# Multi-head latent attention block: query weights loaded two pairs ahead, projection pieces at other heads, first output products moved forward

## The chip, the core and the metric

The kernel runs on one core of a Trainium2 chip. The metric is the device time of one launch in microseconds; smaller is better. Five engines work side by side, each on its own list of instructions in its own order: TensorE (PE in the profile, with its weight loads as PEld), VectorE (DVE), ScalarE (ACT), GpSimd (POOL) and SyncE (SP). SP does no arithmetic here; it issues transfers (DMA). A transfer or an instruction that has to wait holds up all that stands behind it in the list of the same engine.

## The reference

One transformer block on a sequence of 2048 tokens with 512 features: attention with low-rank queries and keys (16 heads, query rank 384, key and value rank 128, 128 plain and 64 rotary features per head), a residual sum and layer norm, then a linear layer with bias, a residual sum and layer norm again. Cut to what matters:

```python
cq = rms_norm(x @ w_qa.T, q_a_ln_w)                  # 2048 x 384
q = (cq @ w_qb.T).reshape(b, s, H, 192)              # 128 plain + 64 rotary per head
q_pe = q_pe * cos + rotate_half(q_pe) * sin
ckv = x @ w_kva.T                                    # 128 latent + 64 rotary, shared by the heads
kv = rms_norm(ckv[..., :128]) @ w_kvb.T              # keys and values of each head
scores = einsum('bhqd,bhkd->bhqk', q_full, k_full) * scale, causal
out = softmax(scores) @ v                            # then @ w_o.T
x = layernorm(x + out)
x = layernorm(x + x @ (w * scale_weight).T + bias)
```

All is float32 in and out. The kernel never builds keys and values per head: the key half of `w_kvb` is multiplied into the query weights once, the value half into the output weights, so scores and values work on the 128-wide latent that all heads share.

## The kernel before, in words

To keep float32 accuracy on a faster matmul, most operands are split in a high and a low part (`split`, L60: a copy on ACT, the difference on DVE), and a product is three matmuls.

The 2048 queries go through in four blocks `b` of 512, and in each block the 16 heads go through as eight pairs `p`. A pair has four query tiles `qt` of 128 queries, so eight steps, called heads below: head 0 is tile 0 of the first head (`j` = 0), head 1 is tile 0 of the second, and so on to head 7. `units` (L607) writes this order out. Block 0 takes a shorter path with a whole tile at a time, mixed with the projections of the input and of the weights; blocks 1 to 3 run in a region where the order on PE and SP is the order of the program (`manual_schedule`, L717), while a planner places the work of ACT, DVE and POOL.

In a head, `head_scores` (L418) computes the scores on PE (L407) into PSUM tiles `s`, the row maximum on DVE (L440), a bias, and the exponential on ACT (L455) into `pr`. `head_probs` (L471) scales and splits them into 16-bit halves `hl` (L476 on ACT, L479 on DVE), and SP transposes them by DMA (L483) into a ring in SBUF. It is a generator that is finished in the course of the next head, so the transpose of a head stands in SP's order after the next head's scores. `values` (L521) multiplies the transposed probabilities with the latent (L532) into a PSUM tile `o`; it runs some tiles later (`lag`), and its result goes through `ot` (L537, ACT) to DRAM (`ot_d`, L284 on POOL in block 0, L292 on SP later).

The queries of the next pair are made meanwhile, in pieces ("fillers") that `fill` (L543) takes one at a time between a head's scores and the values of an earlier tile:

- `project_nope` (L366): two pieces of nine matmuls each (L377), one per head of the pair, from `cq` (the block's 384-wide latent queries) and `wq` (the pair's weights, 768 KB). After the second piece it issues the load of the next pair's `wq` (`load_wq`, L309) into the same, single buffer; after the last pair's it also issues the load of the next block's `cq` and `cs` (`load_block`, L297).
- `project_pe` (L322): for four heads at once, two pieces of nine matmuls (L334) with the products with cosine and sine on DVE (L339). What follows (sums on POOL, copies and differences) is written by the third call, together with the next piece.

A pair with an even number has four pieces, one with an odd number two, the last pair of a block four (the next block's first pair). The heads after which a piece is taken, in block 1 before its last pair: 0, 1, 2, 4 (odd pairs 0, 1); in block 2 after its first pair 0, 1, 3, 5 (odd 0, 1); elsewhere 1, 3, 5, 7 (odd 1, 3). SP's list has the transposes, the loads of `wq`, `wpe`, `cq`, `cs`, and the stores `ot_d`, which `put_in` places.

In the last two pairs of block 3 the loads of the output weights start: `wv` and a quarter `wo0` (1 MB each) at pair 6, `wo1` at pair 7. `value_output` (L172) multiplies them to the combined weights `wvo` of a pair; pairs 0 and 1 are made as pieces of pair 7.

After the last head, `wo2` and `wo3` are loaded (L730), the outstanding values are finished (`finish`, L695), and the last stage begins: per pair, `latent` (L760) loads an `o` tile of the stored results (512 KB) and splits it (`oh`, `ol`), `accumulate` (L771) multiplies it with `wvo` into one of four PSUM tiles `acc` (six matmuls each), and layer norms and the linear layer are worked in between. In this stage only PE's order is written out; SP's is the planner's, which had moved the loads and splits of the first `o` tiles forward into pair 6 of block 3.

Of the kernel before, what the change touches and what calls it, by code (L numbers as in the profile page):

```python
# [11 lines left out]
F32 = mybir.dt.float32  # L12
# [7 lines left out]
P = 128  # L20
# [29 lines left out]
def mla_block(ctx: ExitStack, tc: tile.TileContext, a, out):  # L50
# [258 lines left out]
    def load_wq(b, p):  # L309
        if b == NB:  # L310
            return
        w = state["wq", b, p] = prj.tile([P, 2, LT, 256], F32R, tag="wq", name=f"wq{b}_{p}")
        c0 = (p % 2) * 256
        move(state["queue"], w, wq_d[p // 2][:, :, :, c0 : c0 + 256])
# [7 lines left out]
    def project_pe(b, g, direct=None):  # L322
# [6 lines left out]
        for x in range(2):  # L329
# [10 lines left out]
            if x:  # L340
                if b or g == 3:
                    load_wpe(*((b, g + 1) if g < 3 else (b + 1, 0)))
            yield
# [20 lines left out]
        state["pe", b, g] = pe  # L364

    def project_nope(b, p, direct=None):  # L366
# [5 lines left out]
        for j in range(2):  # L372
# [9 lines left out]
            if j == 1:  # L382
                state["qn", b, p] = qn
                if b or p == NPAIR - 1:
                    load_wq(*((b, p + 1) if p + 1 < NPAIR else (b + 1, 0)))
                if p == NPAIR - 1:
                    load_block(b + 1)
# [186 lines left out]
    wq0 = prj.tile([P, 2, LT, 256], F32R, tag="wq", name="wq0_0")  # L574
# [32 lines left out]
    def units(pool, ring, b):  # L607
        lag = min(ring.shape[1] // (2048 * (b + 1)) - 1, 3)

        for p in range(NPAIR):  # L610
            put_in(True)
            if b and p % 2 == 0 and p + 2 < NPAIR:
                fillers.append(project_pe(b, p // 2 + 1))
            if p + 1 < NPAIR:
                fillers.append(project(b, p + 1) if b == 0 else project_nope(b, p + 1))
            elif b + 1 < NB:
                fillers.append(project(b + 1, 0))
            if b == NB - 1 and p == NPAIR - 2:
                wv = state["wv"] = blk.tile([P, H, P], F32, tag="pe", name="wv")
                nc.sync.dma_start(wv, a["wv"])  # L620
                wo = state["wo"] = [pool.tile([P, 4, HID], F32, tag="wo", name="wo0", bufs=1)]
                nc.sync.dma_start(wo[0], a["wo"][:, 0:4])
            if b == NB - 1 and p == NPAIR - 1:
# [5 lines left out]
                wv, wo = state["wv"], state["wo"]  # L629
# [9 lines left out]
            for qt in range(4):  # L639
# [19 lines left out]
                else:  # L659
                    for j in range(2):  # L660
# [3 lines left out]
                        if (b, p, qt, j) == (1, 0, 0, 0):  # L664
                            half_values()
                            half_values()
                        early = b == 1 and p + 1 < NPAIR
                        if j != early or qt == 0 and (early or b == 2 and p > 0):
                            fill()
# [25 lines left out]
    def finish():  # L695
        flush()
        while vals:
            half_values()

# [10 lines left out]

    ctx_m = ctx.enter_context(ExitStack())
# [4 lines left out]
    state["queue"] = nc.sync  # L716
    with tc.manual_schedule(engines={mybir.EngineType.PE, mybir.EngineType.SP}):  # L717
        for b in range(1, NB):
            with ExitStack() as ctx_s:
# [4 lines left out]
                units(blk13, ring, b)  # L724
        put_in(True)
    state["queue"] = nc.gpsimd
    pcr, wvo, wv, wo = (state[k] for k in ("pcr", "wvo", "wv", "wo"))
    for i, tag in ((2, "pe"), (3, "qn")):
        wo.append(blk.tile([P, 4, HID], F32, tag=tag, name=f"wo{i}"))
        nc.sync.dma_start(wo[i], a["wo"][:, 4 * i : 4 * i + 4])  # L730
    ps_a = ctx.enter_context(tc.tile_pool(name="ps_a", bufs=4, space=PSUM, reuse_waits="tile"))
    finish()
# [10 lines left out]
    ohl = [[pc.tile([P, 4, 256], F32R, name=f"ohl{p}_{i}") for i in range(2)] for p in range(4)]  # L743
# [15 lines left out]

    def latent(b, p, last):  # L760
        o = pcr.tile([P, 4, 256], F32, tag="o", name=f"o{b}_{p}")
        nc.sync.dma_start(o, ot_d[b][p])
        if last and p >= 4:
            oh, ol = ohl[p - 4]
        else:
            oh = pcr.tile([P, 4, 256], F32R, tag="oh", name=f"oh{b}_{p}")
            ol = pcr.tile([P, 4, 256], F32R, tag="ol", name=f"ol{b}_{p}")
        split(o, oh, ol)
        return oh, ol

    def accumulate(acc, p, t, oh, ol):  # L771
        for j in range(2):
            c = slice(j * P, (j + 1) * P)
            for n, (l, i) in enumerate(((oh, 0), (oh, 1), (ol, 0))):
                nc.tensor.matmul(  # L775
                    acc,
                    l[:, t, c],
                    wvo[p][:, i, j, :],
                    start=p == 0 and j == 0 and n == 0,
                    stop=p == NPAIR - 1 and j == 1 and n == 2,  # L780
                )
# [30 lines left out]

    late = []
# [8 lines left out]
    with tc.manual_schedule(engines={ET.PE}):  # L822
        order = [(b, p) for b in range(NB) for p in range(NPAIR)]
        cuts = {order[0]: latent(0, 0, False)}
        for b in range(NB):
            last = b == NB - 1
            accs = [ps_a.tile([P, HID], F32, tag="acc", name=f"acc{b}_{t}") for t in range(4)]
            for p in range(CUT if last else NPAIR):
                nxt = order[NPAIR * b + p + 1]
                cuts[nxt] = latent(*nxt, nxt[0] == NB - 1)  # L830
                for t in range(4):
                    accumulate(accs[t], p, t, *cuts[b, p])
                    if b == 0 and p + 2 < NPAIR and t == 1:
                        heads = [2 * (p + 2) + j for j in range(2)]
                        for _ in value_output(
                            p + 2, wvo[p + 2], [wv[:, h] for h in heads], [wo[h // 4][:, h % 4] for h in heads], ps_f, "ff"
                        ):
                            pass
# [78 lines left out]
```

## Time and profile before

| what | value |
|---|---|
| median of 3 runs | 1662.82 us (1662.26 to 1666.56) |
| time of the profiled execution | 1661.02 us |
| its span | 1659.2 us |
| mean granted clock of TensorE | 0.981 |
| PE busy | 1567.8 us, 94% of the span |
| DVE, ACT, POOL busy | 71%, 56%, 20% |
| mean busy share of the DMA engines, 262 to 1390 us | about 0.78 |
| the same after 1413 us | 0.29 |

Block 0 ends near 257 us, block 1 near 524, block 2 near 909, block 3's last scores near 1384; the last values end at 1412.8. A row of the timeline gives the start, the length and the instruction, and in brackets the idle time of its engine before it with what ended it. A wait row reads "who waited, for whom: total, times, longest". An SP row's length holds the time that the queue took over the instruction, its waits too. PEclk is the clock that TensorE was granted, in tenths; it drops to half for some time around longer gaps.

### The profile page before, as it was taken

The page shows a single profiled execution, that of the slowest core. Times are in us where ns is not written, and L with a number is a line of the kernel's source. Part 1 is how long each engine was busy: PE and PEld are TensorE (multiplying, and loading weights), DVE is VectorE, ACT ScalarE, POOL GpSimd, SP SyncE. Part 2 cuts the span into 40 slices and gives each one's busy share as a digit, 9 for nine tenths or more (in the row PEclk, how much of TensorE's full clock was granted, in tenths as well). Part 3 has the DMA queues.
Part 4 walks back from the last instruction along what each step waited for, and adds up shares of the span by engine and source line. Part 5 has one row for each costly group of instructions (what it writes and reads, how often), then busy time and mean ns, then how long its engine had stood idle before and what let it go on. Part 6 is the DMA issues. An engine that isn't in the chain of part 4 may idle for free. (4 is left out here: it accounts for less than half of the span.)

```text
span 1659.2 us, 24718 instructions
## 1 busy us (share of the span) xinstructions
PE 1567.8 (94%) x9130; PEld 1299.4 (78%) x9130; DVE 1172.6 (71%) x2115; ACT 936.1 (56%) x1647; POOL 330.7 (20%) x404
## 2 busy tenths in 40 slices
PE   8998997999998799999998999999999997999997
PEld 7787876778777678888887888888888785788886
DVE  6777776777777868787786777767767774455464
ACT  5776765565556646666675656666566664312120
POOL 2332424143100505040000310500500000022132
PEclk9999998999999999999999999999999998999999
DMA  6979674878787767878887677787688998333230
GB/s 218 246 213 238 156 194 108 165 163 159 159 193 151 146 141 149 178 153 169 201 180 140 117 160 153 152 159 161 126 158 191 189 179 188 105 108 120 90 121 32
DMA packets 632841, 262.50 MB, mean 158 GB/s; under 512 B 570288, under 2 KB 611120, under 8 KB 631696
## 3 DMA queue, kind: packets, MB, share of 16 engines
q1 hardware_dynamic: 621184, 233.35, 64.7%
q0 software_dynamic: 4768, 17.99, 3.5%
q10 hardware_dynamic: 6768, 9.57, 1.9%
q8 instruction: 72, 1.18, 0.3%
q14 instruction: 49, 0.40, 0.1%
HBM read 83.17 MB, written 35.13 MB: 71 GB/s over the span
## 5 line engine op out<-in xcount | busy, mean ns | idle before, releaser
L407 PE MATMUL s<-Kn,qn 128*128 128x512 f32 (+4 forms) x1920 | 520.7, 377 | 12.2 <-ACT pr L455 10.3
L455 ACT ACTIVATE pr<-s,bias,rq 128x1024 f32<-128x1024 f32 (+3 forms) x320 | 324.1, 1016 | 194.2 <-DVE bias L449 150.4
L532 PE MATMUL o<-ring,V 128*128 128x256 f16 x3252 | 400.7, 277 | 27.7 <-DMA ring<-hl 18.2
L479 DVE SCALAR_TENSOR_TENSOR hl<-pr,inv,hl 128x1024 f16<-128x1024 f32 (+7 forms) x320 | 358.7, 1136 | 83.0 <-ACT hl L476 81.2
L532 PEld LDWEIGHTS <-V 128*128 128x128 f16 x3264 | 307.4, 99 | 117.6 <-issue 61.6
L476 ACT ACTIVATE hl<-pr,inv 128x1024 f16<-128x1024 f32 (+7 forms) x320 | 295.4, 961 | 182.6 <-DMA ring<-hl 74.9
L407 PEld LDWEIGHTS s<-Kn,qn 128*128 128x128 f32 x1920 | 338.7, 190 | 61.1 <-ACT pr L455 16.6
L440 DVE TENSOR_REDUCE neg<-s 128x1 f32<-128x1024 f32 (+3 forms) x320 | 318.5, 995 | 83.9 <-PE s L407 79.9
L407 PE MATMUL s<-Kp,pe 128*128 128x512 f32 (+4 forms) x1280 | 361.0, 363 | 0.0
L407 PEld LDWEIGHTS s<-Kp,pe 128*128 128x128 f32 x1280 | 234.0, 189 | 29.8
L377 PE MATMUL ps_qn<-cq,wq 128*128 128x512 f32 x576 | 151.9, 410 | 23.0 <-DMA wq<-wq_d 15.5
L346 POOL TENSOR_TENSOR prod<-prod 128x512 f32<-128x512 f32 x15 | 19.3, 1288 | 740.7 <-DVE prod L339 740.7
L377 PEld LDWEIGHTS ps_qn<-cq,wq 128*128 128x128 f32 x576 | 111.1, 198 | 47.6 <-issue 12.5
L775 PE MATMUL acc<-wvo,oh 128*128 128x512 f32 x448 | 143.5, 401 | 0.0
L361 POOL TENSOR_TENSOR pe<-prod,ph 32x512 fp32r<-32x512 f32 x76 | 119.7, 1575 | 10.0 <-issue 5.1
L775 PEld LDWEIGHTS acc<-wvo,oh 128*128 128x128 f32 x448 | 83.4, 188 | 20.9 <-issue 2.9
L775 PE MATMUL acc<-wvo,ol 128*128 128x512 f32 x224 | 88.4, 395 | 0.0
L284 POOL DMA_DIRECT2D ot_d<-ot x33 | 18.7, 568 | 293.8 <-ACT ot L537 263.1
L334 PE MATMUL ps_pe<-cq,wpe 128*128 128x512 f32 x288 | 73.2, 400 | 2.3 <-DMA cq<-cq_d 1.6
L537 ACT ACTIVATE ot<-o 128x256 f32<-128x256 f32 x128 | 48.0, 376 | 38.0 <-PE o L532 36.3
L63 ACT ACTIVATE oh<-o 128x1024 fp32r<-128x1024 f32 x28 | 29.6, 1058 | 67.6 <-PE acc L775 53.5
L64 DVE TENSOR_TENSOR ol<-o,oh 128x1024 fp32r<-128x1024 f32 x28 | 38.5, 1376 | 41.3 <-ACT oh L63 41.3
(140 smaller groups left out, 1624.3 us busy)
## 6 DMA issues: line engine op xcount, KB each, us to landing
wq<-wq_d SPq DMA_DIRECT2D x22, 768.0 KB, 5.6
o<-ot_d SPq DMA_DIRECT2D x32, 512.0 KB, 3.3
ot_d<-ot SPq DMA_DIRECT2D x95, 128.0 KB, 2.4
wpe<-wpe_d SPq DMA_DIRECT2D x10, 768.0 KB, 4.8
wq<-wq_d POOLq DMA_DIRECT2D x9, 768.0 KB, 6.2
wq_d<-wst SPq DMA_DIRECT2D x9, 512.0 KB, 4.7
cq_d<-cqst SPq DMA_DIRECT2D x18, 256.0 KB, 3.6
ot_d<-ot POOLq DMA_DIRECT2D x33, 128.0 KB, 2.6
```

What stands on the lines that cost most here:

```text
L64: nc.vector.tensor_tensor(l, ps, h.bitcast(F32), ALU.subtract)
L334: nc.tensor.matmul(ps, w[:, i, lt, x * P : (x + 1) * P], cq[:, k, lt, :], start=n == 0, stop=n == 8)
L361: (nc.gpsimd if not quick or (b, g) == (0, 0) and j % 2 else nc.vector).tensor_tensor(pe[64 + 32 * x : 96 + 32 * x, j, :], rp[q, x, :], ph ...
L377: nc.tensor.matmul(ps, w[:, i, lt, j * P : (j + 1) * P], cq[:, k, lt, :], start=n == 0, stop=n == 8)
L407: nc.tensor.matmul(ps[:, :w], lhs, K[:, i, c0 : c0 + w], start=n == 0, stop=n == 4)
L440: nc.vector.tensor_reduce(neg[:, ti : ti + 1], v, axis=AX.XY, op=ALU.max, negate=True)
L455: nc.scalar.activation(pr[:, c0 : c0 + n * w].rearrange("p (a c) -> p a c", a=n), v, AF.Exp, bias=bias, scale=r, accum_out=sums[:, ti : ti ...
L476: nc.scalar.activation(hl[:, 0, c], pr[:, c], AF.Copy, scale=inv)
L479: nc.vector.scalar_tensor_tensor(hl[:, 1, c], pr[:, c], inv, hl[:, 0, c], ALU.mult, ALU.subtract)
L532: nc.tensor.matmul(ps[:, :256], vt[:, i, k % 4, :], v[:, :, l, k, :], start=n == 0, stop=n == 3 * kts - 1)
L537: nc.scalar.activation(ot, ps[:, :256], AF.Copy)
L775: nc.tensor.matmul(acc, l[:, t, c], wvo[p][:, i, j, :], start=p == 0 and j == 0 and n == 0, stop=p == NPAIR - 1 and j == 1 and n == 2,)
```

## The change

Four things are changed.

1. `wq` has two buffers: pairs with an even number keep the old one, odd pairs of blocks 1 to 3 use one in the pool `blk13` that later holds `wo0`. After the second piece of a pair's projection the weights of the pair after the next are loaded. The weights of pair 1 of block 1 are loaded at the start of the ordered region. `wo0` therefore is loaded at pair 7 of block 3, next to `wo1`.
2. The heads after which a piece is taken are a table, `at`: 0, 2, 4, 6 in even pairs, 2, 5 in odd pairs and pair 6, 0, 1, 3, 5 in pair 7, and 3, 4, 5, 6 in the last pair of block 3. In the first pair of block 1 they are 0, 1, 4, 5, with pair 1's projection first and the values of block 0's last tile after heads 2 and 3.
3. `project_pe` writes its tail with its second piece.
4. After block 3, still in the ordered region, the first `o` tile is loaded between the last two transposes; the products of the first two pairs (`EARLY`, 48 matmuls) are written between the remaining values: the first half of the last-but-one tile stands ahead of them, its second half after six of them, and the last tile after all of them. The output weights of pairs 2 and 3 are then made one after the other at the start of the last stage. `latent` and `accumulate` are moved up unchanged.

```diff
     def load_wq(b, p):
         if b == NB:
             return
-        w = state["wq", b, p] = prj.tile([P, 2, LT, 256], F32R, tag="wq", name=f"wq{b}_{p}")
+        pool, tag = (state["blk13"], "wo") if b and p % 2 else (prj, "wq")
+        w = state["wq", b, p] = pool.tile([P, 2, LT, 256], F32R, tag=tag, name=f"wq{b}_{p}", bufs=1)
...
-            if x:
-                if b or g == 3:
-                    load_wpe(*((b, g + 1) if g < 3 else (b + 1, 0)))
-            yield
+            if x == 0:
+                yield
+            elif b or g == 3:
+                load_wpe(*((b, g + 1) if g < 3 else (b + 1, 0)))
...
         state["pe", b, g] = pe
+        yield
...
-                if b or p == NPAIR - 1:
-                    load_wq(*((b, p + 1) if p + 1 < NPAIR else (b + 1, 0)))
+                if b:
+                    load_wq(*((b, p + 2) if p + 2 < NPAIR else (b + 1, p + 2 - NPAIR)))
+                elif p == NPAIR - 1:
+                    load_wq(1, 0)
...
+            first = (b, p) == (1, 0)
+            if first:
+                fillers.append(project_nope(b, 1))
             if b and p % 2 == 0 and p + 2 < NPAIR:
                 fillers.append(project_pe(b, p // 2 + 1))
+            if first:
+                at = (0, 1, 4, 5)
+            elif p == NPAIR - 1:
+                at = (0, 1, 3, 5)
+            else:
+                at = (2, 5) if p % 2 or p + 2 == NPAIR else (0, 2, 4, 6)
...
             if b == NB - 1 and p == NPAIR - 2:
                 wv = state["wv"] = blk.tile([P, H, P], F32, tag="pe", name="wv")
                 nc.sync.dma_start(wv, a["wv"])
-                wo = state["wo"] = [pool.tile([P, 4, HID], F32, tag="wo", name="wo0", bufs=1)]
-                nc.sync.dma_start(wo[0], a["wo"][:, 0:4])
...
+                wo = state["wo"] = [pool.tile([P, 4, HID], F32, tag="wo", name="wo0", bufs=1)]
+                nc.sync.dma_start(wo[0], a["wo"][:, 0:4])
+                at = (3, 4, 5, 6)
...
-                        if (b, p, qt, j) == (1, 0, 0, 0):
+                        if first and qt == 1:
                             half_values()
-                            half_values()
-                        early = b == 1 and p + 1 < NPAIR
-                        if j != early or qt == 0 and (early or b == 2 and p > 0):
+                        if 2 * qt + j in at:
                             fill()
                         run_values(lag)
...
     with tc.manual_schedule(engines={mybir.EngineType.PE, mybir.EngineType.SP}):
+        load_wq(1, 1)
         for b in range(1, NB):
...
                 units(blk13, ring, b)
+        pcr, wvo, wv, wo = (state[k] for k in ("pcr", "wvo", "wv", "wo"))
+        ps_a = ctx.enter_context(tc.tile_pool(name="ps_a", bufs=4, space=PSUM, reuse_waits="tile"))
+        order = [(b, p) for b in range(NB) for p in range(NPAIR)]
+        cuts = {order[0]: latent(*order[0], False)}
+        for i, tag in ((2, "pe"), (3, "qn")):
+            wo.append(blk.tile([P, 4, HID], F32, tag=tag, name=f"wo{i}"))
+            nc.sync.dma_start(wo[i], a["wo"][:, 4 * i : 4 * i + 4])
+        flush()
+
+        accs = [ps_a.tile([P, HID], F32, tag="acc", name=f"acc0_{t}") for t in range(4)]
+        for p in range(EARLY):
+            cuts[order[p + 1]] = latent(*order[p + 1], False)
+            for t in range(4):
+                if len(vals) > 1:
+                    half_values()
+                accumulate(accs[t], p, t, *cuts[order[p]])
+        while vals:
+            half_values()
         put_in(True)
...
         for b in range(NB):
             last = b == NB - 1
-            accs = [ps_a.tile([P, HID], F32, tag="acc", name=f"acc{b}_{t}") for t in range(4)]
-            for p in range(CUT if last else NPAIR):
+            if b:
+                accs = [ps_a.tile([P, HID], F32, tag="acc", name=f"acc{b}_{t}") for t in range(4)]
+            else:
+                output_weights(2)
+                output_weights(3)
+            for p in range(0 if b else EARLY, CUT if last else NPAIR):
```

## The prediction

> **What bounds the kernel now.** I read the page first: who is busy, and what clock TensorE was granted.
>
> ```profile
> PE 1567.8 (94%) x9130; PEld 1299.4 (78%) x9130; DVE 1172.6 (71%) x2115; ACT 936.1 (56%) x1647; POOL 330.7 (20%) x404
> PEclk9999998999999999999999999999999998999999
> ```
>
> TensorE is the bound: the change removes no matmul, so it can only win TensorE's idle time (some 83 us of gaps) and what the halved clock costs behind a gap. So next, the waits of TensorE alone (us in total, times, longest):
>
> ```profile
> PE o L532 <- DMA ring<-hl: 18.2, 7, 8.6
> PE ps_qn L377 <- DMA wq<-wq_d: 15.5, 4, 11.5
> PE s L407 <- ACT pr L455: 10.3, 13, 2.3
> PE o L532 <- ACT ot L537: 7.5, 5, 3.7
> PE ps_qn L377 <- DVE qn L67: 5.0, 4, 2.3
> PE o L532 <- DMA carry<-hl: 5.0, 1, 5.0
> ```
>
> Four gaps make most of it. The timeline of TensorE places them (start, length, instruction, gap before):
>
> ```profile
> 264.79 2.74 PE L532 MATMUL o<-carry,V 128*128 128x256 f16 x12 [4.97 <-DMA carry<-hl]
> ...
> 296.76 3.42 PE L377 MATMUL ps_qn<-cq,wq 128*128 128x512 f32 x9 [2.75 <-DMA wq<-wq_d]
> ...
> 424.14 1.17 PE L407 MATMUL s<-Kn,qn 128*128 128x320 f32 x3 [2.34 <-ACT pr L455]
> ...
> 584.24 3.99 PE L377 MATMUL ps_qn<-cq,wq 128*128 128x512 f32 x9 [11.53 <-DMA wq<-wq_d]
> ...
> 592.37 2.22 PE L377 MATMUL ps_qn<-cq,wq 128*128 128x512 f32 x9
> ...
> 1404.49 8.30 PE L532 MATMUL o<-ring,V 128*128 128x256 f16 x48 [8.64 <-DMA ring<-hl]
> ```
>
> Rows 4 and 5 also show the clock: the same nine matmuls take 3.99 us behind the gap and 2.22 us later. Last, the queue that issues every load and transpose in order, SP, and the landing that the trace gives for its transposes:
>
> ```profile
> 260.25 2.19 SPq L516 DMA_TRANSPOSE carry<-hl  x1
> ...
> 470.52 0.60 SPq L58 DMA_DIRECT2D cq<-cq_d  x1
> 471.21 0.38 SPq L304 DMA_DIRECT2D cs<-in_csq_dram  x1
> 471.69 5.69 SPq L483 DMA_TRANSPOSE ring<-hl  x1
> ...
> 574.72 3.61 SPq L483 DMA_TRANSPOSE ring<-hl  x1
> 578.42 0.56 SPq L58 DMA_DIRECT2D wq<-wq_d  x1
> ...
> 1388.43 8.31 SPq L483 DMA_TRANSPOSE ring<-hl  x1
> ```
>
> The load at 578.42 stood behind a transpose whose probabilities came only then, and landed 5.8 us later: that is the 11.53. A big load just ahead of a transpose slows it: 5.69 us of issue instead of 1.5 at 471.69, 8.31 instead of 4.5 at 1388.43.
>
> **The change, part by part.** The sum is made against the profiled execution: span 1659.2, 1.8 around it, 1661.0 in all; the median of the runs shown, 1662.8, stands 1.8 higher.
>
> *Query weights two pairs ahead: gains.* After the change, the second-buffer loads stand in SP 37 to 98 us before their use (the old trace's times at the new places); before, five had under 6 us of room. So the gap at 584.24 goes with its slow piece: 11.53 + (3.99 - 2.22) = 13.3. At 296.76: 2.75 + (3.42 - 2.22) + 0.57 for nine value matmuls (1.73, then 1.16) = 4.5. At 1220.20: 0.7. What is late next: in block 2 TensorE then runs 100% busy for 200 us with landings 13 us early, so nothing.
>
> *The load moved to the start of block 1: a loss.* wq for pair 1 leaves the POOL queue (issued at 251.8) and goes on SP behind the carry transpose, which ends at 262.44; the median landing of this load is 5.6 us, so 268.1. The order now puts this pair's first projection directly after the first scores, at 259.8. Before, TensorE went on at 264.79. Loss 3.3; ends 0 (shortest landing 2.4) and 6.2 (longest 8.5). Value matmuls of the carry tile, now later, cover nothing here, since TensorE works in order. Pair 2's load takes its place on POOL and has 60 us. SP's next load, for pair 3, waits for the second projection piece; the transpose behind it waits for VectorE longer (278.8).
>
> *Pieces spread: gains.* In block 1 the pieces went after heads 0,1 or 0,1,2,4; now 2,5 or 0,2,4,6. Gaps of a second piece right behind the first (0.37 + 2.27 + 0.43 + 0.79 + 1.12 = 5.0) should go: two heads, some 8 us, lie between them now. The gap at 424.14 (2.34 + 1.4 of slow matmuls) is the exponentials' pace; I take a quarter. Together 6; ends 0 (the work of DVE, 75% busy there, is only shifted) and 8.7. Same reason in block 2 (0.84 at 814.31), and 0.6 at 1287.63, where one of two 1 MB loads leaves: 1.4.
>
> *Pieces spread: losses.* The last piece of pair 6 now comes after head 5, not 1, and it frees cq, whose 1536 KB reload for the next block goes out with the next wq and cs right behind. cq is needed by the first piece of pair 7, after head 0. In block 1: from head 5's scores to that piece TensorE has 2.1 + 1.2 + 2.4 + 0.6 + 2.4 + 0.9 + 1.8 = 11.4 us. SP reaches the loads 8.3 us after head 5's scores (transposes of the same head in pairs 1 to 3), and cq lands 9.9 us after the transpose ahead of it (469.7 to 479.6): 18.2. A new wait of 6.8, with 1.7 of slow clock 8.5. It stands in for the gaps that the early reload and the crowded pair 7 made (2.06 + 1.27 + 2.74 + 1.4 slow + 1.04 + 0.9 = 9.4), of which I leave 2, for the rope tail on DVE (5.57 us) still comes there: net loss 1; ends a gain of 9.4 (cq in time, all gone) and a loss of 8.5. At the end of block 2 the same count gives 7.5 to 8 us of room for 9.9: loss 2, ends 0 and 5.
>
> *A page against the row.* The Trainium skill, "DMA: Bandwidth & Descriptors", section "Bandwidth", speaks against such bursts: 1 MB takes 6.15 us. Estimated from it, wq and cq (2.25 MB) need 13.8 us, not the row's 9.9, and the sum would be 4 us higher. No run here shows such a burst on an otherwise idle queue. I go by the row.
>
> *wo0 at pair 7 instead of 6.* Both 1 MB loads now precede the transpose of head (6, 7), which has no room: at 1346.63 TensorE already waited 0.17 for it. With two such loads ahead the transpose at 1276.48 landed after 11.0, with one that at 1336.63 after 9.9. New landing 1337.1 + 11.0 = 1348.1; TensorE comes at 1345.6 (one output-weight piece of 0.86 moved away): 2.3 more, and 1.5 of slow clock: 3.8; ends 0 and 5.
>
> *The rope tail emitted with its second piece*: POOL does it 70 us before its use; nothing.
>
> *First output products between the last values.* Old: gap 8.64, then 48 matmuls in 8.30 us, at 45-in-5.07 worth 5.4. New: 36 more matmuls (8.4 us) stand before them. But their input, o0, used to be loaded at 1297; it is now in SP's order, after the first of the last two transposes: 1389.5 + 4.5 = 1394.0, landed some 4 us later (3.4 to 4.6 at 1297), split 1.1 + 1.3 on ACT and DVE: products from 1399. TensorE waits from 1390.4 and, half of this at slow clock, has done 24 values and four products at 1410.6. The second o0 tile is behind the last transpose, which now has 0.5 + 2 MB ahead: issued 1395.4, ends 1404, o lands 1409, split by 1411.4. Products to 1416.5, last values to 1421.7. Old: 1412.8 plus the 36 products (8.4), 1421.2. Then four output-weight pieces in a row through two buffers: 0.9 of wait. Loss 1.4; ends a gain of 8 (o0 in time) and a loss of 5.
>
> **Sum.** Gains 13.3 + 4.5 + 0.7 + 6 + 1.4 = 25.9; losses 3.3 + 1 + 2 + 3.8 + 1.4 = 11.5. 1661.0 - 14.4 = 1646.6, and as a median of runs (up to 1.8 higher) 1647.
>
> *The clock, row against page.* Gaps of 2.75 and 2.34 us were followed by slow matmuls. The Trainium skill, "TensorE: Matmul & The Clock Gate", section "HAM oscillation", sets the harmful gap at about 3.4 us; by it 1.8 + 1.4 of the old slow time had not arisen and the wo wait would cost 1.5 less. The rows decide.
>
> **Rivals.**
> 1. *The moved loads are hidden.* For: SP's lag shrinks when TensorE stalls less. Against: the room of cq is below zero on the old trace's clock. Gains 25.9, loss 3.3 at the start, and 6 won at the tail: 1632.4, with 1.8 about 1634.
> 2. *Only the wq gains stay.* Block 1's gaps reappear behind the exponentials, and cq, wo, tail cost 8.5 + 4 + 5 + 4, start 3.3, against 19.9: 1665.9. For: the probabilities trail the scores by 9 to 14 us all through block 1. Then same.
> 3. *Slower: score tiles wait for the exponentials in blocks 2 and 3*, because a piece now stands behind the first head of a tile and none behind the second, whose masked reduction is the later one. Price: 1.34 us, the longest such wait there, in each of 16 pairs: 21.4, so 1661.0 - 14.4 + 21.4 = 1668, 1670 as a median. It decides from 14.4 / 16 = 0.9 us a pair. Against: the number of heads without a piece is unchanged, and all such waits in these blocks together are below 10 us now.
>
> **How the numbers follow.** My forecast 0.55, rival 1 0.20, rival 2 0.15, rival 3 0.10. About 0.3% (5 us) is what a measurement of this kernel can tell from no change. Faster: forecast, rival 1 and a third of rival 2, 0.80; same: 0.09; slower: rival 3 and the tail of 2, 0.11. Range 1632 (rival 1) to 1661 (all losses at their ends without block 1's gains, from which the wq gains still leave something).
>
> **What will show it.** Right: no wait of ps_qn for wq over 1 us after block 1's start; a wait of ps_pe for cq of 4 to 8 us near 480; a start gap near 8 us waiting for wq; a tail gap of 7 to 9 us waiting for the first split o0. Wrong: cq in time, products with no wait, or more than 15 us of s waiting for pr.

## The result and the profile after

The changed kernel takes 1685.01 us (median of four runs, 1684.76 to 1685.38) against 1662.8 us (1662.26 to 1666.56): ratio 1.0129, 95% interval 1.0111 to 1.0146. It is slower by 22 us where 16 us of gain were forecast, and outside the range of 1632 to 1661 us. The profiled execution took 1684.76 us, its span is 1683.0 us, 23.8 more than before. From the page of the changed kernel, who is busy and the granted clock:

```profile
PE 1576.2 (94%) x9130; PEld 1305.6 (78%) x9130; DVE 1170.7 (70%) x2115; ACT 935.9 (56%) x1647; POOL 333.3 (20%) x402
...
PEclk9999998999989999999999999999999998999999
```

TensorE does the same 9130 matmuls; its busy time grew by 8.4 us, as more of them ran behind gaps at a halved clock, and its gaps from 83.6 to 99.2 us. TensorE's waits in the changed kernel (us in total, times, longest):

```profile
PE s L411 <- ACT pr L459: 25.3, 16, 3.0
PE ps_pe L335 <- DMA cq<-cq_d: 12.3, 3, 7.9
PE acc L737 <- ACT oh L63: 11.5, 2, 9.9
PE o L536 <- ACT ot L541: 8.8, 7, 3.8
PE ps_qn L379 <- DMA wq<-wq_d: 8.1, 1, 8.1
PE o L536 <- DMA ring<-hl: 6.8, 3, 4.4
...
PE ps_wo L176 <- DVE wvo L67: 4.4, 3, 2.7
```

The waits that the change aimed at did fall: the wait for the query weights fell from 15.5 to 8.1 us, all of it the load moved to the start of block 1, and the transposes' wait (ring) from 18.2 to 6.8. But 15 us more of scores (s) wait for exponentials, and three waits are as good as new: cq (12.3), the first output products (acc, 11.5), the output weights (ps_wo, 4.4).

To see where the time went I took from both traces when each pair's first score matmul starts. The difference, after minus before, grows or shrinks in each stretch by (us):

| stretch | predicted | measured |
|---|---|---|
| block 0 | 0 | +1.8 |
| block 1, pair 0 (load at the start) | +3.3 | +2.5 |
| block 1, pairs 1 to 6 (gap at 296.76, spread pieces) | -10.5 | -5.2 |
| block 1, pair 7 (cq late) | +1 | +5.2 |
| block 2, pair 0 | 0 | +5.6 |
| block 2, pair 1 (gap at 584.24) | -13.3 | -8.8 |
| block 2, pairs 2 to 6 | -0.8 | -0.7 |
| block 2, pair 7 (cq late) | +2 | +3.0 |
| block 3, pair 0 | 0 | +3.0 |
| block 3, pairs 1 to 5 | -0.7 | +3.6 |
| block 3, pair 6 | -0.6 | -2.5 |
| block 3, pair 7 (wo0) | +3.8 | +6.1 |
| from the last scores to the end | +1.4 | +10.2 |
| sum | -14.4 | +23.8 |

TensorE's timeline shows the largest of them (start, length, instruction, gap before; a row that shows fewer than nine matmuls of a projection, such as the x6 here, ends at the edge of its view):

```profile
269.36 2.93 PE L379 MATMUL ps_qn<-cq,wq 128*128 128x512 f32 x6 [8.09 <-DMA wq<-wq_d]
...
494.89 4.18 PE L335 MATMUL ps_pe<-cq,wpe 128*128 128x512 f32 x9 [7.85 <-DMA cq<-cq_d]
...
529.65 0.79 PE L411 MATMUL s<-Kn,qn 128*128 128x384 f32 x3 [1.35 <-ACT pr L459]
...
534.58 1.33 PE L411 MATMUL s<-Kn,qn 128*128 128x384 f32 x3 [2.92 <-ACT pr L459]
...
586.66 0.79 PE L411 MATMUL s<-Kn,qn 128*128 128x384 f32 x3 [2.39 <-ACT pr L459]
...
1357.42 5.30 PE L536 MATMUL o<-ring,V 128*128 128x256 f16 x24 [4.39 <-DMA ring<-hl]
...
1412.56 1.22 PE L737 MATMUL acc<-wvo,oh 128*128 128x512 f32 x2 [9.91 <-ACT oh L63]
...
1425.29 0.73 PE L737 MATMUL acc<-wvo,oh 128*128 128x512 f32 x2 [1.63 <-ACT oh L63]
...
1447.28 1.12 PE L176 MATMUL ps_wo<-wo,wv 128*128 128x512 f32 x2 [2.75 <-DVE wvo L67]
```

Rows 1, 2, 6 and 7 were forecast, with their places: 8.1 us for wq (some 8 forecast), 7.85 for cq (6.8), 4.39 for the transpose (2.3), 9.91 for the split o tile (8.6). Rows 3 to 5 and the second o tile's 1.63 us were not, and of the waits of the last row's kind (4.4 us in all) only 0.9.

### The profile page after: what moved, and what is told of

The parts are those of the page before. It is cut to its first block, busy times and chain, and to the rows that moved or that the text cites. A ratio compares the mean times of both kernels' runs of the same rounds, so it can differ in the third digit from the quotient of the medians.

```text
span 1683.0 us, 24761 instructions
## 1 busy us (share of the span) xinstructions
PE 1576.2 (94%) x9130; PEld 1305.6 (78%) x9130; DVE 1170.7 (70%) x2115; ACT 935.9 (56%) x1647; POOL 333.3 (20%) x402
## 3 DMA queue, kind: packets, MB, share of 16 engines
q8 instruction: 72, 1.18, 0.3%
## 5 line engine op out<-in xcount | busy, mean ns | idle before, releaser
L411 PE MATMUL s<-Kn,qn 128*128 128x512 f32 (+4 forms) x1920 | 522.6, 378 | 27.2 <-ACT pr L459 25.3
L737 PE MATMUL acc<-wvo,oh 128*128 128x512 f32 x448 | 146.1, 408 | 11.5 <-ACT oh L63 11.5
L737 PEld LDWEIGHTS acc<-wvo,oh 128*128 128x128 f32 x448 | 84.8, 192 | 33.4 <-ACT oh L63 12.2
L335 PE MATMUL ps_pe<-cq,wpe 128*128 128x512 f32 x288 | 76.9, 415 | 12.3 <-DMA cq<-cq_d 12.3
L335 PEld LDWEIGHTS ps_pe<-cq,wpe 128*128 128x128 f32 x288 | 56.2, 200 | 24.1 <-issue 8.1
```

The costliest lines, as they stand in the source:

```text
L335: nc.tensor.matmul(ps, w[:, i, lt, x * P : (x + 1) * P], cq[:, k, lt, :], start=n == 0, stop=n == 8)
L411: nc.tensor.matmul(ps[:, :w], lhs, K[:, i, c0 : c0 + w], start=n == 0, stop=n == 4)
L737: nc.tensor.matmul(acc, l[:, t, c], state["wvo"][p][:, i, j, :], start=p == 0 and j == 0 and n == 0, stop=p == NPAIR - 1 and j == 1 and n ...
```

## The experiments

Times are given as the ratio to the kernel before in the same group of runs, with its 95% interval, and as that ratio times 1662.8 us. "Steps" are those of the table above, "tail" the stretch from the end of the last scores to the end of the span in the profiled execution: 274.8 us before, 285.0 after. A step comes from one profiled execution of each kernel: block 0, which the change hardly touches, differs by +0.6 to +4.5 us, and the tail as the changed kernel has it (runs 2, 7, 8, 9 and 10 keep it, run 4 has it alone) by +5.3 to +10.3. The profiled execution before, 1661.0 us, lies low among all runs of that kernel (1660.0 to 1671.3), so steps add up to less gain than the times: -18.6 against -22.6 us in run 11.

**1. The old tail under the changed rest.** The products, the o tiles, the loads of wo2 and wo3 and the output weights of pairs 2 and 3 go back to their old places behind the manual order:

```diff
-        cuts = {order[0]: latent(*order[0], False)}
-        for i, tag in ((2, "pe"), (3, "qn")):
...
-        for p in range(EARLY):
-            cuts[order[p + 1]] = latent(*order[p + 1], False)
-            for t in range(4):
-                if len(vals) > 1:
-                    half_values()
-                accumulate(accs[t], p, t, *cuts[order[p]])
...
         put_in(True)
     state["queue"] = nc.gpsimd
...
+    for i, tag in ((2, "pe"), (3, "qn")):
...
+    finish()
```

> The changed kernel with its last part undone: the first output products and their o tiles go back behind the manual order, wo2 and wo3 are loaded where they were before; the two query-weight buffers, the places of the pieces and wo0 at pair 7 stay. Theory A (each part has its own price, read off the trace after: 10.7 us from the last scores to the last stage's start belong to the new tail): 1685 - 10.7 = 1674 us. Rival B (the tail is late only because the work before it is late, and would cost the predicted 1.4 us by itself): the tail's loss stays in another wait, 1683 to 1685 us.

Measured: 1.0071 (1.0049 to 1.0094), 1674.6 us; tail 273.2 us. Theory A holds: the tail carries 10 us of its own.

**2. The old places, with the two buffers and the new tail.**

```diff
-            if first:
-                at = (0, 1, 4, 5)
-            elif p == NPAIR - 1:
-                at = (0, 1, 3, 5)
-            else:
-                at = (2, 5) if p % 2 or p + 2 == NPAIR else (0, 2, 4, 6)
+            at = (0, 1, 2, 4, 6) if b == 1 and p + 1 < NPAIR else (0, 1, 3, 5, 7) if b == 2 and p else (1, 3, 5, 7)
-            if first:
-                fillers.append(project_nope(b, 1))
```

The edit also takes back part 3 of the change, the rope tail (not shown). The last pair of block 3 keeps 3, 4, 5, 6, here and in run 3.

> The changed kernel with the pieces back at the old heads (block 1: after heads 0, 1, 2, 4, 6; block 2: 0, 1, 3, 5, 7; block 3: 1, 3, 5, 7; the piece of the rope tail as before, the first pair's projection back behind the rope projection); two query-weight buffers, wo0 at pair 7 and the new tail stay. Theory A (the places cost the late cq and the score tiles that wait for exponentials; the second buffer alone keeps its gain): 1662.8 - 13.3 - 4.5 - 0.7 for the three gaps, + 6.1 for wo0 + 10.7 for the tail = 1661 us, no wait for cq over 1 us. Rival C (the 1 MB loads now issued two pairs ahead slow the transposes beside them wherever the pieces stand): the losses stay, about 1680 us.

Measured: 0.9994 (0.9977 to 1.001), 1661.8 us; tail 285.1. Theory A again, and rival C falls: the loads two pairs ahead do no harm by themselves. The new places, with the first pair's order and the rope tail, cost 23 us, the largest single part of the miss. (Runs 11 and 12 keep that order and that tail and are the fastest, so neither is the loss by itself.) That theory A's total fits is partly luck: the two gaps for wq did not simply go, and wo0 cost 3.0 us in pair 7 instead of 6.1. TensorE's timeline in this run:

```profile
302.51 1.65 PE L378 MATMUL ps_qn<-cq,wq 128*128 128x512 f32 x6 [3.12 <-DVE qn L67]
...
576.37 3.18 PE L378 MATMUL ps_qn<-cq,wq 128*128 128x512 f32 x9 [2.25 <-ACT ot L540]
```

At both places the same projection now waits for its two accumulator buffers, to be emptied by DVE or by ACT. The step of pair 1 of block 2 is -9.4 here and -8.8 in the changed kernel; I had counted 13.3.

**3. The two buffers alone**: old places and old tail, wo0 at pair 7.

```diff
-        w = state["wq", b, p] = prj.tile([P, 2, LT, 256], F32R, tag="wq", name=f"wq{b}_{p}")
+        pool, tag = (state["blk13"], "wo") if b and p % 2 else (prj, "wq")
+        w = state["wq", b, p] = pool.tile([P, 2, LT, 256], F32R, tag=tag, name=f"wq{b}_{p}", bufs=1)
...
-                    load_wq(*((b, p + 1) if p + 1 < NPAIR else (b + 1, 0)))
+                    load_wq(*((b, p + 2) if p + 2 < NPAIR else (b + 1, p + 2 - NPAIR)))
```

> The kernel before with the two query-weight buffers alone (and wo0 at pair 7, since its buffer holds query weights until then): old places, old tail. Theory A: 1662.8 - 18.5 + 6.1 = 1650 us. Rival C (loads slow the transposes): gains of 18.5 eaten by some 14 us of new waits for ring, 1665 us.

Measured: 0.9964 (0.9949 to 0.9979), 1656.8 us: faster than the kernel before, between the two theories. Pair 1 of block 2 gives -9.2 and pair 1 of block 1 nothing (+2.2), for the reason seen in run 2 (here a wait of 3.89 us at 303.24 for DVE); wo0 takes 4.8 in pair 7, where TensorE waits 4.18 us for a transpose.

**4. The new tail alone** on the kernel before (the inverse of run 1's edit).

> The kernel before with the new tail alone: the first output products between the last values, o tiles and wo2 and wo3 loaded in the manual order, two pieces of output weights moved behind the last values; one query-weight buffer, old places, wo0 at pair 6. Theory A (the tail's 10.7 us are its own): 1662.8 + 10.7 = 1673.5 us, with a wait of acc for the split o tile near 9 us and some 4 us of waits of ps_wo for the emptied buffers. Rival B (the tail costs what was predicted, 1.4 us; the rest came from the lateness ahead of it): 1664 us.

Measured: 1.0037 (1.0025 to 1.0049), 1669.0 us; the profiled execution is the longest of its eight runs, with a tail of 284.8 us, acc waiting 8.30 and 3.04 us for split o tiles and ps_wo 3.4 us in all. By the times the tail costs 6 us, by the trace 10; 1.4 is excluded either way. It needs none of the other parts.

**5. The o tiles early**: both are requested before the third query tile of the last pair.

```diff
             for qt in range(4):
+                if (b, p, qt) == (NB - 1, NPAIR - 1, 2):
+                    cuts.update({q: latent(*q, False) for q in ((0, 0), (0, 1))})
...
-        cuts = {order[0]: latent(*order[0], False)}
```

> The changed kernel with the o tiles of the first two output products requested on SP before the third query tile of the last pair's scores, instead of behind the first of the last transposes; nothing else. Theory A (the 9.9 us wait of acc is the o load that stands behind transposes in SP's order; split in time, the 36 extra products and the last-but-one values reach to the landing of the last transpose, 1402.7 + 2.1 + 2.8 + 7 x 2.06 = 1422 against 1421.1): minus 9 to 10 us, 1675.5 us, no wait of acc over 1 us. Rival B (the wait only moves to the last transpose, since wo2 and wo3 ahead of it hold it up): minus 0 to 3 us.

Measured: 1.0044 (1.0028 to 1.006), 1670.1 us, some 14 us under the changed kernel, more than expected; tail 267.5 us, 7 less than before the change. Against run 1, which has the old tail, it is 4.5 us faster by the times, and runs 11 and 12, with the same early o tiles, have tails 3.0 and 3.8 us shorter than before: the gain over the old tail is 3 to 7 us. SP's queue in the changed kernel shows what the o load stood behind, and in front of:

```profile
1402.20 4.90 SPq L487 DMA_TRANSPOSE ring<-hl  x1
1407.15 0.57 SPq L724 DMA_DIRECT2D o<-ot_d  x1
1407.82 0.86 SPq L766 DMA_DIRECT2D wo<-in_wo_dram  x2
1408.77 10.30 SPq L487 DMA_TRANSPOSE ring<-hl  x1
1419.12 0.57 SPq L292 DMA_DIRECT2D ot_d<-ot  x1
1419.78 0.88 SPq L724 DMA_DIRECT2D o<-ot_d  x2
```

TensorE had finished all that was ready at 1402.65; the first o tile was requested 4.5 us after that, the second another 12.6 us later, behind the slow transpose. In run 5 TensorE's timeline has in the same place:

```profile
1405.99 0.73 PE L739 MATMUL acc<-wvo,oh 128*128 128x512 f32 x2 [0.68 <-ACT pr L459]
...
1421.72 5.41 PE L536 MATMUL o<-ring,V 128*128 128x256 f16 x48 [1.88 <-DMA ring<-hl]
```

The 36 matmuls of the products fill almost the whole time until the last transpose lands, and the 48 value matmuls behind them run in 5.41 us. So the products do cover the wait for the transposes; it was the place of the o loads in SP's order that kept them from it.

**6. Output weights taken one pair later**, so that two pieces stand together and not four.

```diff
                 output_weights(2)
-                output_weights(3)
...
-                    if b == 0 and p + 2 < NPAIR and t == 1:
-                        output_weights(p + 2)
+                    if b == 0 and p + 1 < NPAIR and t == 1:
+                        output_weights(p + 1)
```

> The changed kernel with the output weights of pair 3 taken one pair later, and so every later pair, so that two pieces stand together instead of four. Theory A (the waits of ps_wo for the emptied buffers, 0.9 + 2.75 + 0.7 us, and the slow matmuls after them come from four pieces in a row through two buffers, emptied by ACT and DVE behind the feed-forward weights): minus 4.4 to 7.5 us, 1679 us. Rival B (the emptying waits for the feed-forward weights' load, whenever the pieces come, and the wait moves to the next pair's pieces): 1685 us.

Measured: 1.0129 (1.0104 to 1.0154), 1684.3 us, nothing by the times, as rival B has it. In the trace the waits of ps_wo are gone, but the products of the same pair wait 1.08 and 0.93 us for the weights; the tail is 279.8, no better than the 280.1 to 280.4 of runs 7 and 10, where the pieces stand as in the changed kernel. So the stretch varies by 5 us between executions, and what the four pieces cost by themselves stays open. What holds them up is visible in the changed kernel, on DVE and on ACT:

```profile
1438.93 1.41 DVE L67 SCALAR_TENSOR_TENSOR wvo<-ps_wo,kvln_o,wvo 128x512 fp32r<-128x512 f32 x2 [4.98 <-ACT wvo L66]
1444.09 0.69 DVE L795 TENSOR_TENSOR fraw<-fraw,fsc 128x512 f32<-128x512 f32 x1 [3.75 <-DMA fsc<-in_fsc_dram]
1445.87 0.69 DVE L795 TENSOR_TENSOR fraw<-fraw,fsc 128x512 f32<-128x512 f32 x1 [1.08 <-DMA fraw<-in_fw_dram]
1446.47 0.75 DVE L67 SCALAR_TENSOR_TENSOR wvo<-ps_wo,kvln_o,wvo 128x512 fp32r<-128x512 f32 x1
```

```profile
1440.90 0.69 ACT L66 ACTIVATE wvo<-ps_wo,kvln_o 128x512 fp32r<-128x512 f32 x1 [1.38 <-PE ps_wo L176]
1444.82 0.63 ACT L63 ACTIVATE fw<-fraw 128x512 fp32r<-128x512 f32 x1 [3.23 <-DVE fraw L795]
```

The planner has put feed-forward weight preparation (fraw, fw) between two emptyings of ps_wo. DVE stands 3.75 us for the scale row fsc, whose load was issued only at 1437.38 and landed at 1444.07, and 1.08 us more for the next raw weights; the next emptying stands behind both, ends at 1447.22, and TensorE goes on at 1447.28.

**7. Pair 6's pieces early**, so that cq's reload goes out in time.

```diff
-                at = (2, 5) if p % 2 or p + 2 == NPAIR else (0, 2, 4, 6)
+                at = (0, 1) if p + 2 == NPAIR else (2, 5) if p % 2 else (0, 2, 4, 6)
```

> The changed kernel with the pieces of pair 6 after heads 0 and 1 instead of 2 and 5 in every block, so that cq is free one to one and a half heads... of pair 6 earlier (36 us in block 1) and its reload goes out then; pair 7 keeps its places. Theory A (the late cq makes both the waits for cq, 7.85 and 2.92 us, and the lateness of the exponentials in the next block's first pair, 5.6 and 3.0 us): minus 12 to 17 us, about 1671 us. Rival D (the waits of the scores for the exponentials in the next block's first pair come from pair 7 having no piece behind its last two heads): the waits for cq go, the waits at 530, 535 and 886 stay, minus 4 to 8 us, about 1679 us.

Measured: 1.0089 (1.0069 to 1.011), 1677.6 us. Both waits for cq went; the waits of the scores stayed, 0.68 and 2.67 us where block 2 begins (1.35 and 2.92 in the changed kernel) and 0.67, 1.95 and 0.95 in block 3's first pair, as rival D has it. (The wait at 886, which the expectation put there too, lies in pair 7 of block 2, and stayed as well.) The gain at pair 7 of block 1 (7.5 us) is mostly eaten in pair 6 (5.5 us), where the second piece again stands right behind the first. TensorE's timeline:

```profile
458.09 2.24 PE L379 MATMUL ps_qn<-cq,wq 128*128 128x512 f32 x9
...
468.23 2.07 PE L379 MATMUL ps_qn<-cq,wq 128*128 128x512 f32 x4 [5.44 <-DVE qn L67]
...
533.66 1.16 PE L411 MATMUL s<-Kn,qn 128*128 128x384 f32 x3 [2.67 <-ACT pr L459]
```

**8. Pair 7's pieces back at the odd heads.**

```diff
-                at = (0, 1, 3, 5)
+                at = (1, 3, 5, 7)
```

> The changed kernel with the pieces of pair 7 in blocks 0 to 2 back after heads 1, 3, 5, 7 instead of 0, 1, 3, 5; pair 6 keeps 2 and 5. cq is then needed one head (8 us in block 1, 14 in block 2) later, just as it lands. Theory A: as with pair 6 early, both waits go: 1671 us. Rival D: also 1671 us, but here the waits of the scores at 530, 535 and 886 go whatever cq does; told from A by the run with pair 6 early.

Measured: 1.0086 (1.0057 to 1.0114), 1677.1 us. In block 1 cq is still waited for, 5.73 us: a head there lasts 4 us (a pair of eight 31 to 36), not the 8 that I had counted, so the need moved by too little. In block 2 the wait went. The scores' waits where block 2 begins became 2.36 and 0.86 us instead of 1.35 and 2.92, and those in block 3's first pair stayed (0.66, 1.93 and 0.95 us): a piece behind pair 7's last heads is not what they lack, and rival D's second half falls too.

**9. Odd heads in block 3 and in pair 0 of block 2.**

```diff
+            if b == NB - 1 or (b, p) == (2, 0):
+                at = (1, 3, 5, 7)
```

> The changed kernel with the pieces of all of block 3 and of the first pair of block 2 after the odd heads (1, 3, 5, 7) instead of the even ones (0, 2, 4, 6) or 2 and 5; the output-weight pieces of the last pair stay. Theory E (score tiles wait for exponentials where no piece stands behind a query tile's second head): the steps of pair 0 of block 2 (+5.6 us against the kernel before), pair 0 of block 3 (+3.0) and pairs 1 to 5 of block 3 (+3.6 together) go, 1685 - 12 = 1673 us. Rival G (pair 0 of a block is late because the block before it ended late, with cq and the rope tail): only the 3.6 us of pairs 1 to 5 go, 1681 us.

Measured: 1.0064 (1.0039 to 1.0089), 1673.4 us. The steps of block 3's pair 0 and pairs 1 to 5 went from +3.0 and +3.6 to 0.0 and -1.9; that of block 2's pair 0 stayed, +4.5. So theory E holds in block 3. In block 2 the step stays, as rival G has it, though not by G's cause, the late cq: in run 7 cq was in time and the step was +7.4. That the time fits theory E's 1673 is partly luck: where that step stayed, pair 7 of block 3 gained (+3.5 instead of +6.1), and the tail was 8.1 instead of 10.2. TensorE's waits for exponentials from 910 to 1270 us (block 3 from its first pairs to pair 5), in the kernel before:

```profile
PE s L407 <- ACT pr L455: 3.4, 6, 1.0
```

in the changed kernel:

```profile
PE s L411 <- ACT pr L459: 9.5, 8, 1.9
```

and in run 9:

```profile
PE s L411 <- ACT pr L459: 2.9, 6, 0.8
```

**10. The two buffers given to the other pairs**: pair 1 of block 1 in the old buffer, loaded on the POOL queue in time; pair 2 in the new one, on SP; wo0 back at pair 6.

```diff
-        pool, tag = (state["blk13"], "wo") if b and p % 2 else (prj, "wq")
+        pool, tag = (state["blk13"], "wo") if b and p % 2 == 0 and (b, p) != (1, 0) else (prj, "wq")
...
-        load_wq(1, 1)
+        load_wq(1, 2)
```

> The changed kernel with the two query-weight buffers given to the other pairs: odd pairs (and pair 0 of block 1) in the old buffer, even pairs in the new one. So the weights of block 1's pair 1 are loaded on the POOL queue during block 0 as before the change, those of pair 2 on SP at the start of block 1, and wo0 finds its buffer free at pair 6. Theory A (the start gap of 8.09 us and the ring wait of 4.39 us with the slow matmuls behind it are the two loads that the change moved): the start gap goes whole, 8 us (the piece covers the carry transpose too), and 6 us of pair 7: 1671 us. Rival B (the transposes at pair 7 are late anyway, the start gap turns back into the old 4.97 us for the carry tile): minus 3 us, 1682 us.

Measured: 1.0026 (1.0012 to 1.004), 1667.1 us, some 17 under the changed kernel; in the trace pair 0 of block 1 gains 10.0 and pair 7 of block 3 gains 5.3. Theory A holds: both losses were the two loads that the change had moved. The start then even beats the kernel before by 7.5 us in that step, since the projection fills the old wait of 4.97 us for the carry tile. TensorE's timeline, with no gap ahead of either piece:

```profile
263.95 2.54 PE L379 MATMUL ps_qn<-cq,wq 128*128 128x512 f32 x9
...
267.80 2.20 PE L379 MATMUL ps_qn<-cq,wq 128*128 128x512 f32 x9
...
271.61 0.83 PE L538 MATMUL o<-carry,V 128*128 128x256 f16 x6
```

**11. What the runs point to, together**: buffers as in run 10, o tiles as in run 5, and these places:

```diff
             elif p == NPAIR - 1:
-                at = (0, 1, 3, 5)
+                at = (1, 3, 5, 7)
+            elif p == NPAIR - 2:
+                at = (0, 2) if b < 3 else (1, 3)
+            elif b == 1:
+                at = (2, 5) if p % 2 else (0, 2, 4, 6)
             else:
-                at = (2, 5) if p % 2 or p + 2 == NPAIR else (0, 2, 4, 6)
+                at = (0, 1, 3, 5, 7) if b == 2 and p else (1, 3, 5, 7)
```

(the output-weight pieces of the last pair stay after heads 3 to 6).

> What the runs so far point to, together: the swapped buffers, the early o tiles, the spread places only in block 1's pairs 1 to 5, pair 6 after heads 0 and 2 (cq reload early, pieces two heads apart), pair 7 and block 3 after the odd heads, block 2 as before the change. Theory A by its prices against the kernel before: start 5, gap at 296 and spread in block 1 5, gap at 584 9, tail 6: 1662.8 - 25 = 1638 us. Rival B (what is freed in one place is waited for in the next, as at 584, where 13.3 us became 8.8): half of it, 1650 us.

Measured: 0.9864 (0.984 to 0.9888), 1640.2 us: 23 us faster than the kernel before, some 44 faster than the changed one. Theory A was 2 us off, its terms by more: the steps give 7.4 us at the start where it has 5, and 3.0 in the tail where it has 6.

**12. Run 11 with block 1's old places in pairs 1 to 6.**

```diff
+            elif b == 1 and p + 1 < NPAIR:
+                at = (0, 1, 2, 4, 6)
...
-            elif b == 1:
-                at = (2, 5) if p % 2 else (0, 2, 4, 6)
```

> The combined kernel with the pieces of block 1's pairs 1 to 6 back after heads 0, 1, 2, 4, 6; nothing else. Theory H (the spread's gain in block 1 is a loan: TensorE runs ahead of the exponentials there and waits for them at the end of the block and in block 2's first pair; with the old places pairs 1 to 6 of block 1 are some 4 us slower and pair 7 with pair 0 of block 2 some 5 to 6 us faster): 1640 us, the same within 3 us. Rival I (the spread's gain of 4 us lasts, and the lateness in block 2's first pair comes from elsewhere): 1646 us, and the step of pair 0 of block 2 stays.

Measured: 0.9856 (0.983 to 0.9882), 1638.9 us, not to be told from run 11 by the times (1636.3 to 1647.6 against 1640.5 to 1646.3). The steps, of one profiled execution each, tell where: pairs 1 to 6 of block 1 give -3.5 in run 11 and -0.2 in run 12; pair 7 and the first two pairs of block 2 give -3.3 and -10.2, and pair 0 of block 2 alone +3.7 and +0.1. That is theory H: the spread's gain in block 1 is a loan, paid back where block 1 ends and block 2 begins. That it is paid back is shown by the steps; through what is read off the waits alone. TensorE's waits from 480 to 620 us, in run 11:

```profile
PE s L413 <- ACT pr L461: 3.8, 2, 2.3
PE o L538 <- DVE prod L340: 2.6, 2, 2.2
PE o L538 <- ACT ot L543: 2.3, 1, 2.3
PE ps_qn L379 <- ACT ot L543: 2.2, 1, 2.2
```

and in run 12, where the scores' wait is lower and DVE's product is no longer waited for:

```profile
PE s L413 <- ACT pr L461: 2.3, 1, 2.3
PE ps_qn L379 <- ACT ot L543: 2.3, 1, 2.3
PE o L538 <- DMA ring<-hl: 2.1, 1, 2.1
PE o L538 <- ACT ot L543: 1.3, 2, 1.1
```

## Why the prediction was wrong

Of the 38 us between the sum (-14.4) and the trace (+23.8), by its steps:

- **"Pieces spread: gains", 6 us in block 1, and "pieces spread: losses", 1 and 2 us for cq: the step that failed most.** With the 1.4 us in blocks 2 and 3 the spread was to win 4 us; against run 2 it costs 23. By the steps of run 2, 3.2 of these lie at the start of block 1, nothing net in its pairs 1 to 7, 5.1 and 4.1 in the first and last pair of block 2, and 10.6 in block 3. It failed in three ways. First, the gaps that were to go were put down to pieces standing too close, and were taken for TensorE's own loss. Run 12 shows the gain to be paid back in the three pairs that follow: TensorE got ahead, and then stood for exponentials and for DVE. Second, the cq wait was sized well, 7.85 us against 6.8 with 2.0 of slow matmuls against 1.7 (cq landed 10.3 us after the transpose ahead of its load, against the row's 9.9), but it was to "stand in for" 7.4 of 9.4 us of old gaps, and stood in for some 4.6: the step was +5.2, not +1. Run 7 takes the wait away and shows most of the cost reappear in pair 6. Third, the steps of the first pairs of blocks 2 and 3 (5.6 and 3.0 us), where scores wait for exponentials, were in no term of the sum. Block 3's was the pieces' place in that pair (run 9). Block 2's is +0.5 with all the old places (run 2) and +0.1 in run 12; an early cq, pair 7's places or pair 0's own, changed singly, leave +7.4, +3.8 and +4.5 of it. So it comes out of block 1, as run 12 against run 11 shows (+0.1 against +3.7); which of block 1's pairs hands it on is not settled.
- **"In block 2 TensorE then runs 100% busy ..., so nothing [is late next]": wrong.** At the gap of 584.24 I looked at the stretch behind it and not at what had used the 11.5 us of standstill to catch up. 8.8 came of 13.3, and most of the rest is waits for exponentials (2.39) and for emptied o buffers (1.62); with other places for emptied accumulators (run 2). The same at 296.76: the wait for wq gave way to one of 3.1 to 3.9 us for DVE (runs 2 and 3).
- **Rival 3, dismissed because "the number of heads without a piece is unchanged": its mechanism is real in block 3.** It cost 0.6 to 1.1 us in pairs 1 to 4 and 3.0 in pair 0, and nothing in pairs 2 to 6 of block 2. The number was the wrong thing to count; in block 3 it is which of a query tile's two heads has the piece behind it (run 9). Why the same places cost nothing in most of block 2, no run shows. As a price for 16 pairs (1.34 each) it was too high, and its total of 1670 too low, since it stood alone.
- **"First output products between the last values", 1.4 us: mechanism right, sizes wrong; 10.2 measured (6 by the times of run 4, 10 by those of run 1).** The wait for the first o tile was 9.91 against 8.6. The last values ended 39.1 us behind the last scores; the forecast was 37.3 (1421.7 less 1384.4). Most of the rest is the output-weight pieces: 0.9 us of waits forecast, 4.4 measured, and 2.8 us of slow clock behind the last of them (the twelve matmuls from 1450.22 on take 5.57 us, the next twelve 2.79). I had counted the buffers and not asked what else DVE and ACT would have in their queues by then. The end of the range that I gave this term, a gain of 8 with "o0 in time", is near what the early o tiles brought: 7 in run 5, 3.0 and 3.8 in runs 11 and 12.
- **wo0 next to wo1 at pair 7, 3.8 us: right, under-sized, 6.1.** The transpose landed 12.2 us after its issue, not 11.0, and TensorE waited 4.39 us. Run 10 takes it back to 0.8. With the old places the same loads cost 3.0 and 4.8 us (runs 2 and 3).
- **The load at the start of block 1, 3.3 us: right, 2.5**, with 8.09 us of gap where 8 were named. It is the load together with the new order that costs: in run 2 pair 1's projection comes later, and the same load costs nothing (-0.7).
- **The gaps at 814.31 and 1220.20, and the transposes beside loads two pairs ahead**: as forecast. The wait at 1220.20 is one for exponentials now (0.90), part of block 3's loss; up to the last pair TensorE's waits for transposes over 1 us are 2.42, 1.18 and 4.44 us in run 2, as the 2.06, 1.27 and 4.32 of the kernel before.
- **The rivals.** Rival 1 fell with cq and wo0. Rival 2, only the wq gains stay, names part of what happened, gains of block 1 that go again in waits for exponentials, but its own numbers fall short: ahead of the last pair its terms (3.3 at the start, 8.5 and 4 for cq, against 19.9) come to a gain of 4 us where 7.4 were lost, and it puts 9 on wo0 and the tail where 16.3 were measured.

Of the forecast's signs of being wrong one came: "more than 15 us of s waiting for pr", and there were 25.3. The range was too narrow for another reason: its losses were bounded one by one, each by the rows next to it, while the losses where block 1 ends and block 2 begins move from one wait to another (runs 7, 8 and 12) and cannot be bounded one by one.

## What to carry to other kernels

A gap that goes is worth only what lies between it and the next thing that was late: before counting 13 us, ask which engine used the standstill to catch up, and what it would be waited for without it. Moving a filler changes the pace of the engine that it fills between, so a gain in one block must be followed to the point where another engine's queue catches up; compare the kernels pair by pair, not gap by gap. And when work is moved forward, its loads must move with it in the issuing queue: the early products lost 6 to 10 us, most of it because their input stood behind a transpose, and won 3 to 7 as soon as it stood in front.

## What the runs showed of the clock

Short gaps halve TensorE's clock only sometimes. The changed kernel and run 5 differ only from the last pair on, and both wait 2.92 us for the same exponentials in block 2's first pair. The granted clock (PEclk, third figure from the right) in the four microseconds that follow, in the changed kernel:

```profile
534.58:538.58 4.00, 4.00 (x11) 3.51 (x12) 0.30 (x3) 0.77 (x1) 0.00 (x0) 0.50 1.20 228
```

and in run 5:

```profile
536.90:540.90 4.00, 4.00 (x24) 3.35 (x24) 0.30 (x3) 0.67 (x1) 0.00 (x0) 1.00 1.17 230
```

11 matmuls against 24 in the same four microseconds. Over the 14 profiled executions of this case, behind block 0, the clock was below 0.8 after none of 74 gaps of 1.0 to 1.6 us, after 1 of 22 of 1.6 to 1.9 us, after 65 of 107 of 1.9 to 3.2 us, and after all 60 longer ones. The Trainium skill, "TensorE: Matmul & The Clock Gate", section "HAM oscillation — how this bites in real kernels", names about 3.4 us as the gap to avoid; here the slow clock stood behind every gap above 3.2 us, but already behind 65 of the 107 between 1.9 and 3.2 us. So the slow matmuls behind a gap of 2 to 3 us, some 1.5 us each in the forecast, are a chance and not a price.
